# Layer 0's cross-attention: the reciprocals of the softmax sums moved behind the second pair's maxima

## The chip, the cores and the metric

The kernel runs on one core of a Trainium2 chip. The metric is device time in microseconds (us) of one execution; three executions of the kernel before were timed and their median is the number to compare with. A separate execution was profiled, and every duration below comes from that one. The engines are named as in the profile: PE (matrix multiplies), PEld (weight loads of the same engine), DVE (vector engine), ACT (scalar engine), POOL (GpSimd) and SP (issues DMAs).

## The reference, cut to what matters

The model is a two-layer decoder on `x` of shape (32, 100, 256) with a context `ctx_512` of shape (32, 361, 128). Each layer has a self-attention, a cross-attention and a feed-forward part. Only layer 0's cross-attention is touched:

```python
def _L0_xattn_ref(x, z, Wq, Wkv, Wo):          # 16 heads of 16 channels
    Q = (x @ Wq.T).reshape(B, xN, 16, 16)
    KV = (z @ Wkv.T).reshape(B, zN, 2, 16, 16)
    K, V = KV[:, :, 0], KV[:, :, 1]
    attn = jnp.einsum('bqhd,bkhd->bhqk', Q, K) * 16 ** -0.5
    attn = jax.nn.softmax(attn, axis=-1)
    O = jnp.einsum('bhqk,bkhd->bqhd', attn, V).reshape(B, xN, 256)
    return O @ Wo.T

x = x + _L0_xattn_ref(_layernorm(x), ctx_512, L0_xattn_Wq, L0_xattn_Wkv, L0_xattn_Wo)
```

For each of the 32 batches there are 16 heads, 100 queries and 361 context positions. The softmax needs the row maximum over the 361 positions, the exponentials, their sum, and a division of the weighted values by that sum.

## The kernel before, in words

`l0_xattn` treats a batch in two steps of eight heads each, so there are 64 steps, numbered `M` from 0; step `M` is batch `M // 2`, half `c = M % 2`. Eight heads are handled as two groups `j` of four heads. The loop is software-pipelined over three steps: in iteration `M` the scores of step `M` are computed and their maxima taken, the transposed scores and exponentials of step `M - 1` are made, and the values of step `M - 2` are summed and divided.

PE's order is the order written in the loop (a manual schedule). In one iteration PE does:

1. `maxima(M - 1)`: two transposes (L621), after which DVE adds the negated maxima to the queries (L623, tile `q`, here called the add of the maxima).
2. `scores(M, 0)`: four score matmuls into four PSUM banks; DVE takes the negated maximum of each bank with one reduction (L614). This is the first half.
3. `turned(M - 1, 0)`: twelve matmuls into four banks that give the shifted scores transposed; ACT takes four exponentials (L635), and POOL adds the three context chunks of the exponentials (L639, L640, tile `es`), for the sums.
4. `values(M - 2)`: 24 matmuls for the weighted values (L649) and 8 for the sums (L656), all into one bank. ACT copies the bank to SBUF (L661, tile `zs`), DVE takes the reciprocal of the sums (L662), POOL multiplies the values with it (L664, tile `zT`).
5. `scores(M, 1)` with four more reductions on DVE (L614): the second half.
6. `turned(M - 1, 1)` with four exponentials and POOL's two adds.
7. The extras, in the order 0, 2, 1 of a list of three: for `c = 0` the first keys of the next batch (`keys`, two ACT copies L586), the output projection of a finished tile of 128 rows, where there is one (`out`: DVE's add L241, then BN statistics L177 and L180), and two chunks of the next batch's values (`vals`, four ACT copies L599); for `c = 1` the other keys, the queries of the next four batches in every other pair of batches (`queries`, two ACT copies L579), and the last chunk of values. After them, in some steps, come the turn of a normalised tile (`norm_turn`, its copy L130 on ACT or L131 on DVE by turns) and the gate and routing work of the next feed-forward part, whose small operations run on DVE (L1401 to L1465).

All of this shares eight PSUM banks under one tag, handed out in turn. A matmul group gets the bank that was handed out eight banks earlier, and waits until that one has been read. Counted in that order, the keys take the bank of the first score matmul of the second half, so PE starts the keys only when DVE has done the first of the second half's four reductions; the second extra takes the bank of the second, and so on.

The engines other than PE run what was recorded for them in the order in which the program was built, each engine in order, waiting on the others by semaphores. On DVE the recorded order of one iteration before the change is: add of the maxima (L623), four reductions of the first half, the reciprocal (L662), four reductions of the second half, and then what the extras need (L241, L177, L180 or L131). On POOL it is: the two adds of `turned(M - 1, 0)`, the multiplication by the reciprocals (L664), the two adds of `turned(M - 1, 1)`. The helper `self.depend(instruction, [others], why)` adds a dependency that the data does not ask for.

Of the kernel before, what the change touches and what calls it, by code (L numbers as in the profile page):

```python
# [13 lines left out]
ALU = mybir.AluOpType  # L14
AX = mybir.AxisListType
# [64 lines left out]
class Kernel:  # L80
# [430 lines left out]
    def l0_xattn(self):  # L511
        nc, tc, a = self.nc, self.tc, self.a
        with ExitStack() as st:
# [54 lines left out]
            def load(b):  # L568
                ctx[b] = pool.tile([CD, LP], F32, tag="cT", name="cT", bufs=3)
                nc.sync.dma_start(ctx[b], a["ctxT"][:, b, :])  # L570

            def queries(b0, c):
                if c == 0:
                    q[b0 // 4] = pool.tile([P, 2, 2, 4 * T], F32, tag="qT", name="qT")
                pm = self.bank_t()[:, : 4 * T]
                self.mm(pm, [(wq[:, k, c * P : (c + 1) * P], self.xn_of(k, b0, 4)) for k in range(NK)])
                t = q[b0 // 4]
                for j in range(2):
                    nc.scalar.activation(t[:, c, j, :], pm, AF.Copy, scale=quarter[:, j : j + 1])  # L579

            def keys(b, c):
                pm = self.bank_t()[:, :L]
                self.mm(pm, [(wk[:, c * P : (c + 1) * P], ctx[b][:, :L])])
                t = ks[b % 3]
                for j in range(2):
                    nc.scalar.activation(  # L586
                        t[:, c, j, :L], pm, AF.Identity, bias=one[:, j : j + 1], scale=own[:, j : j + 1]
                    )

            def vals(b, c0, n):  # L590
                pm = self.bank_t()[:KC, : n * D].rearrange("p (c d) -> p c d", c=n)
                for i in range(n):
                    c = c0 + i
                    self.mm(pm[:, i, :], [(ctx[b][:, c * KC : (c + 1) * KC], wv)])
                pv = pm.rearrange("p c (h j d) -> p c h j d", j=2, d=16)
                v = vs[b % 3][:, c0 : c0 + n].rearrange("p c (h j) e -> p c h j e", j=2)
                for j in range(2):
                    for i in range(n):
                        nc.scalar.copy(v[:, i, :, j, 16 * j : 16 * j + 16], pv[:, i, :, j, :])  # L599

            def rows_of(r):
                return slice(32 * r, 32 * r + 32)


            def scores(M, j):
                b, c = divmod(M, 2)
                cols = slice((b % 4) * T, (b % 4 + 1) * T)
                ps = [self.bank("r")[:T, :L] for _ in range(4)]
                for r in range(4):
                    self.mm(ps[r], [(q[b // 4][rows_of(r), c, j, cols], ks[b % 3][rows_of(r), c, j, :L])])  # L610
                m = ms[M % 3]
                for r in range(4):
                    o = 32 * r + 16 * (1 - j)
                    nc.vector.tensor_reduce(m[:, j, o : o + 1], ps[r], AX.X, ALU.max, negate=True)  # L614

            def maxima(M):
                b, c = divmod(M, 2)
                cols = slice((b % 4) * T, (b % 4 + 1) * T)
                pt = self.bank_t()[:, : 2 * T].rearrange("p (j t) -> p j t", j=2)
                for j in range(2):  # L620
                    nc.tensor.transpose(pt[:, j, :], ms[M % 3][:, j, :], self.ident[:T, :T])  # L621
                q2[M] = pool.tile([P, 2, T], F32, tag="q2", name="q2")
                self.after = nc.vector.tensor_tensor(q2[M], pt, q[b // 4][:, c, :, cols], ALU.add)  # L623

            def turned(M, j):
                b, c = divmod(M, 2)
                ps = [self.bank("r")[:KC, : NKC * T] for _ in range(4)]
                for i in range(NKC):
                    for r in range(4):
                        self.mm(ps[r][:, i * T : (i + 1) * T], [(  # L630
                            ks[b % 3][rows_of(r), c, j, i * KC : (i + 1) * KC], q2[M][rows_of(r), j, :]
                        )])
                t = e[M, j] = pool.tile([KC, 4, NKC, T], F32, tag="e", name="e", bufs=5)
                for r in range(4):
                    nc.scalar.activation(t[:, r], ps[r].rearrange("p (c t) -> p c t", c=NKC), AF.Exp)  # L635

                n = L - 2 * KC
                s = es[M, j] = pool.tile([KC, 4, T], F32, tag="es", name="es", bufs=4)
                nc.gpsimd.tensor_tensor(s, t[:, :, 0, :], t[:, :, 1, :], ALU.add)  # L639
                nc.gpsimd.tensor_tensor(s[:n], s[:n], t[:n, :, 2, :], ALU.add)  # L640

            def values(M):
                b, c = divmod(M, 2)
                pz = self.bank_t()[:, : 2 * T].rearrange("p (s t) -> p s t", s=2)
                for j in range(2):
                    t = e.pop((M, j))
                    for i in range(NKC):
                        for r in range(4):
                            nc.tensor.matmul(  # L649
                                pz[rows_of(r), 0, :], lhsT=vs[b % 3][:, i, 8 * c + 2 * r + j, :],  # L650
                                rhs=t[:, r, i, :], start=(j == 0 and i == 0), stop=(j == 1 and i == NKC - 1),
                            )
                for j in range(2):
                    t = es.pop((M, j))
                    for r in range(4):
                        nc.tensor.matmul(  # L656
                            pz[rows_of(r), 1, :], lhsT=ones[:, j, :], rhs=t[:, r, :],
                            start=(j == 0), stop=(j == 1),
                        )
                zs = pool.tile([P, 2, T], F32, tag="zs", name="zs")  # L660
                nc.scalar.copy(zs, pz)  # L661
                nc.vector.reciprocal(zs[:, 1, :], zs[:, 1, :])  # L662
                for z, cols in self.z_parts(b):
                    nc.gpsimd.tensor_tensor(z[:, c, :], zs[:, 0, cols], zs[:, 1, cols], ALU.mult)  # L664

# [17 lines left out]
            def extras(b):  # L683

                k0, k1, v0, v1, o, x = [None] * 6
                if b + 1 < NB:
                    k0, k1 = (lambda: keys(b + 1, 0)), (lambda: keys(b + 1, 1))
                    v0, v1 = (lambda: vals(b + 1, 0, 2)), (lambda: vals(b + 1, 2, 1))
                if b > 1 and tile_of(b - 2) is not None:
                    o = lambda: out(tile_of(b - 2))  # L690
                b0, i = b // 4 * 4, b % 4
                if i < 2 and b0 + 4 < NB:
                    x = lambda: queries(b0 + 4, i)
                return k0, v0, o, k1, v1, x
# [11 lines left out]
            with tc.manual_schedule(engines={mybir.EngineType.PE}):  # L706
                load(0)
                load(1)
                for c in range(2):
                    queries(0, c)  # L710
                for c in range(2):
                    keys(0, c)
                vals(0, 0, 2)
                vals(0, 2, 1)
                last = 2 * NB
                for M in range(last + 2):
                    b, c = divmod(M, 2)
                    if c == 0:
                        if b + 2 < NB:
                            load(b + 2)  # L720
                        ex = extras(b)
                    if 0 < M <= last:
                        maxima(M - 1)
                    if M in norms:
                        f, *at = norms[M]
                        f(*at)
                    for j in range(2):

                        if M < last:
                            scores(M, j)  # L730
                        if 0 < M <= last:
                            turned(M - 1, j)
                        if j == 0 and M > 1:
                            values(M - 2)
                    for i in (0, 2, 1):
                        if ex[3 * c + i]:
                            ex[3 * c + i]()
                    if M not in norms or len(later) > 3:
                        for _ in range(1 + (len(later) > 3)):
                            if later:  # L740
                                later.popleft()()
                out(NF - 1)
                while later:
                    later.popleft()()
# [1260 lines left out]
```

## Time and profile before

| quantity | value |
|---|---|
| median of three runs | 3155.25 us (3146.28, 3155.25, 3155.63) |
| profiled execution: its own time | 3155.59 us |
| profiled execution: span of the instructions | 3153.6 us |
| granted PE clock over the span | 0.981 |
| busy over the span: PE / PEld / DVE / ACT / POOL | 96% / 72% / 57% / 45% / 29% |
| layer 0's cross-attention in the trace | about 587 to 1092 us, 505 us |
| in that stretch, busy PE / PEld / DVE / ACT / POOL | 474.8 / 367.3 / 362.1 / 330.9 / 294.2 us |
| reciprocals L662 | 64, median 778 ns, first at 602.5 us, last at 1089.5 us |
| reductions L614 | 512, median 523 ns |

The profiled execution's own time lies 2.0 us above its span; that is what stands around the first and last instruction. In the stretch of 505 us PE is idle for about 30 us, and every other engine for much more.

### The profile page before, as it was taken

The numbers are of one execution on the slowest core, as the hardware profiler recorded it, in microseconds if no ns is written. First come the engines' busy times: TensorE is split into PE (matmuls) and PEld (weight loads), VectorE is DVE, ScalarE is ACT, GpSimd is POOL, SyncE is SP. The second block draws the span as 40 slices with busy tenths as digits, with TensorE's granted clock in tenths as the row PEclk, the third lists the DMA queues.
The fourth block names the chain that finished last, engine by engine and source line by source line (L and its number), as shares of the span: only waits on it lengthen the run. The fifth ranks groups of instructions, "written<-read, shape, count | busy, mean of one in ns | idle before, by whom it ended". The sixth has DMA issues, their size and how long they took to land. (4 is left out here: it accounts for less than half of the span.)

```text
span 3153.6 us, 67966 instructions
## 1 busy us (share of the span) xinstructions
PE 3013.7 (96%) x26832; PEld 2261.1 (72%) x26832; DVE 1811.1 (57%) x4686; ACT 1406.8 (45%) x4361; POOL 926.3 (29%) x1048
## 2 busy tenths in 40 slices
PE   8999999999999899999998999999999999998983
PEld 7777777677777658888875677777777777776572
DVE  6666666577777622222227876656666666665443
ACT  5555554566666511222232234545545555454220
POOL 3222221465555451000016420021211212122474
PEclk9999999999999999999998999999999999999996
DMA  8850000000000033554541000010000000000387
GB/s 311 305 197 1 1 1 1 18 14 14 14 14 14 16 129 132 202 192 179 201 153 55 14 5 6 8 41 24 15 11 11 11 11 10 9 10 15 109 204 183
DMA packets 130105, 225.86 MB, mean 72 GB/s; under 512 B 40525, under 2 KB 108421, under 8 KB 122992
## 3 DMA queue, kind: packets, MB, share of 16 engines
q1 hardware_dynamic: 98704, 127.32, 12.6%
q0 software_dynamic: 27792, 90.81, 8.8%
q8 instruction: 215, 3.52, 0.5%
q10 hardware_dynamic: 3280, 3.28, 0.3%
q14 instruction: 114, 0.93, 0.1%
HBM read 153.77 MB, written 113.61 MB: 85 GB/s over the span
## 5 line engine op out<-in xcount | busy, mean ns | idle before, releaser
L1651 POOL DMA_INDIRECT x_d<-xr,slot x200 | 194.5, 972 | 775.3 <-DVE kT L131 243.7
L444 ACT ACTIVATE wBx<-ps_t,m 100x361 f32<-100x361 f32 x512 | 280.8, 560 | 259.7 <-DVE m L441 234.2
L136 PE MATMUL ps_t<-xnT,wA 128*128 128x200 f32 x1536 | 300.6, 340 | 1.9 <-DMA wA<-in_wq 1.3
L136 PEld LDWEIGHTS ps_t<-xnT,wA 128*128 128x128 f32 x1536 | 260.0, 192 | 37.4 <-issue 19.5
L441 DVE TENSOR_REDUCE m<-ps_t 100x1 f32<-100x361 f32 x512 | 241.2, 526 | 79.3 <-PE ps_t L136 77.2
L136 PE MATMUL ps_t<-xT,w 128*128 128x256 f32 x1276 | 283.2, 381 | 0.7 <-ACT xT L130 0.7
L136 PEld LDWEIGHTS ps_t<-xT,w 128*128 128x128 f32 x1276 | 240.0, 190 | 41.7 <-issue 9.3
L614 DVE TENSOR_REDUCE m<-ps_t 100x1 f32<-100x361 f32 x512 | 235.5, 517 | 18.1 <-PE ps_t L136 18.0
L338 POOL TENSOR_TENSOR e<-e,rz 100x400 f32<-100x400 f32 x128 | 109.5, 856 | 407.1 <-DVE rz L337 397.6
L635 ACT ACTIVATE e<-ps_t 121x300 f32<-121x300 f32 x512 | 173.9, 426 | 123.5 <-PE ps_t L136 123.4
L334 ACT ACTIVATE e<-s,m 100x100 f32<-100x100 f32 x512 | 186.1, 365 | 20.8 <-DVE m L328 20.1
L136 PE MATMUL ps_t<-wA,zT 128*128 128x256 f32 x800 | 188.0, 388 | 3.8 <-DVE zT L883 3.0
L136 PE MATMUL ps_t<-kT,qT 64*100 64x361 f32 x1024 | 190.1, 488 | 0.9 <-ACT wBx L444 0.9
L639 POOL TENSOR_TENSOR es<-e 121x400 f32<-121x400 f32 x128 | 132.4, 1034 | 197.0 <-ACT e L635 196.8
L136 PE MATMUL ps_t<-cT,wA 128*128 128x361 f32 x512 | 188.5, 492 | 1.5 <-SPq L1250 1.5
L453 PEld LDWEIGHTS ps_t<-ident,wBx 100*121 100x121 f32 x1536 | 178.1, 186 | 12.7 <-issue 5.7
L136 PE MATMUL ps_t<-wA,cT 128*121 128x512 f32 x384 | 184.9, 593 | 0.6 <-ACT wBx L444 0.6
L453 PE MATMUL ps_t<-ident,wBx 100*121 100x100 f32 x1536 | 185.3, 270 | 0.0
L136 PEld LDWEIGHTS ps_t<-wA,zT 128*128 128x128 f32 x800 | 152.1, 193 | 33.3 <-issue 4.7
L1332 DVE TENSOR_TENSOR h<-ps_t,g 128x256 f32<-128x256 f32 x145 | 61.2, 425 | 199.4 <-ACT g L1331 199.4
L131 DVE COPY eT<-ps_t 121x300 f32<-121x300 f32 x339 | 146.7, 461 | 30.6 <-PE ps_t L453 26.4
L471 PE MATMUL ps_z<-eT,v 121*64 121x100 f32 x3072 | 161.0, 254 | 0.3 <-issue 0.3
(301 smaller groups left out, 5810.6 us busy)
## 6 DMA issues: line engine op xcount, KB each, us to landing
x_d<-fill SPq DMA_DIRECT2D x16, 1284.0 KB
we<-in_wexp SPq DMA_DIRECT2D x32, 384.0 KB
cT<-in_ctxT SPq DMA_DIRECT2D x64, 181.5 KB
xe<-x_d SPq DMA_DIRECT2D x32, 321.0 KB
xe_d<-zero SPq DMA_DIRECT2D x8, 1024.0 KB
xe<-xe_d SPq DMA_DIRECT2D x29, 256.0 KB
y_d<-y SPq DMA_DIRECT2D x29, 256.0 KB
sum<-fill SPq DMA_DIRECT2D x10, 640.0 KB
```

The costliest lines, as they stand in the source:

```text
L131: return self.nc.vector.tensor_copy(out, in_)
L136: self.nc.tensor.matmul(out, lhsT=l, rhs=r, start=(i == 0), stop=(i == n - 1))
L334: nc.scalar.activation(t[:, i, :], s[:, i, :], AF.Exp, bias=m[:, i : i + 1], accum_out=rz[:, i : i + 1])
L338: nc.gpsimd.tensor_tensor(t[:, h, :], t[:, h, :], self.last(rz[:, h], T), ALU.mult)
L441: lay.after = nc.vector.tensor_reduce(m, ps[i], AX.X, ALU.max, negate=True)
L444: nc.scalar.activation(t[:, :L], ps[i], AF.Exp, bias=m, accum_out=sums[b][:, h : h + 1])
L453: nc.tensor.transpose(pt[:, c, :], e[n, i][:, c * KC : (c + 1) * KC], self.ident[:T, :T])
L471: nc.tensor.matmul(out, lhsT=v, rhs=eT[n, i][:, c, :], start=first, stop=last)
L614: nc.vector.tensor_reduce(m[:, j, o : o + 1], ps[r], AX.X, ALU.max, negate=True)
L635: nc.scalar.activation(t[:, r], ps[r].rearrange("p (c t) -> p c t", c=NKC), AF.Exp)
L639: nc.gpsimd.tensor_tensor(s, t[:, :, 0, :], t[:, :, 1, :], ALU.add)
L1651: got = nc.gpsimd.indirect_dma_start(out=self.x1_d[:, :], out_offset=bass.IndirectOffsetOnAxis(ap=slot[:, j, k : k + 1], axis=0), in_=xr[: ...
```

## The change

The reciprocal and the multiplication that follows it leave `values` and become a function of their own, `divided`, which is called once both halves of the scores have been recorded. The reciprocal gets a dependency on the last reduction of the second half. In the last two iterations there are no scores any more, and there the order stays as it was. Nothing is added or left out in the computation.

```diff
@@ scores(M, j)
                 for r in range(4):
                     o = 32 * r + 16 * (1 - j)
-                    nc.vector.tensor_reduce(m[:, j, o : o + 1], ps[r], AX.X, ALU.max, negate=True)
+                    got = nc.vector.tensor_reduce(m[:, j, o : o + 1], ps[r], AX.X, ALU.max, negate=True)
+                return got
@@ values(M)
                 zs = pool.tile([P, 2, T], F32, tag="zs", name="zs")
                 nc.scalar.copy(zs, pz)
-                nc.vector.reciprocal(zs[:, 1, :], zs[:, 1, :])
+                return zs
+
+            def divided(M, zs, after):
+                b, c = divmod(M, 2)
+                got = nc.vector.reciprocal(zs[:, 1, :], zs[:, 1, :])
+                if after is not None:
+                    self.depend(got, [after.ins], "behind the maxima, whose banks are waited for")
                 for z, cols in self.z_parts(b):
                     nc.gpsimd.tensor_tensor(z[:, c, :], zs[:, 0, cols], zs[:, 1, cols], ALU.mult)
@@ the loop over M
                     for j in range(2):
-                        if M < last:
-                            scores(M, j)
+                        got = scores(M, j) if M < last else None
                         if 0 < M <= last:
                             turned(M - 1, j)
                         if j == 0 and M > 1:
-                            values(M - 2)
+                            zs = values(M - 2)
+                    if M > 1:
+                        divided(M - 2, zs, got)
```

In the built program this moves 62 of the 64 reciprocals on DVE from in front of the second half's four reductions to behind them. The order on PE, ACT, POOL and SP is the same as before, instruction by instruction.

## The prediction

> **What bounds the kernel.** I read the page first, for the bound and the place of the touched lines.
>
> ```profile
> PE 3013.7 (96%) x26832; PEld 2261.1 (72%) x26832; DVE 1811.1 (57%) x4686; ACT 1406.8 (45%) x4361; POOL 926.3 (29%) x1048
> L614 DVE TENSOR_REDUCE m<-ps_t 100x1 f32<-100x361 f32 x512 | 235.5, 517 | 18.1 <-PE ps_t L136 18.0
> ```
>
> PE bounds; DVE, which the change touches, is 57% busy, so what counts is PE's idle time that DVE ends. Second, the waits of PE from 590 to 1080 us (total us, times, longest):
>
> ```profile
> PE ps_t L136 <- DVE m L614: 21.7, 63, 1.8
> PE ps_t L649 <- DVE m L614: 2.7, 4, 0.9
> ```
>
> The first line is most of PE's 30 us idle in this stage, and comes about once per step. Third, the timeline, for where it lies. Columns: start, duration, engine, line, operation, and in brackets the idle time before and its releaser.
>
> ```profile
> 704.50 0.87 PE L136 MATMUL ps_t<-k,qT 32*100 32x361 f32 x8
> ...
> 708.04 0.42 DVE L241 TENSOR_TENSOR x_sb<-ps_t,x_sb 128x256 f32<-128x256 f32 x1 [0.52 <-PE ps_t L136]
> ...
> 708.97 0.87 PE L136 MATMUL ps_t<-k,qT 32*100 32x361 f32 x8
> 709.08 0.37 DVE L623 TENSOR_TENSOR q<-ps_t,qT 128x200 f32<-128x200 f32 x1
> ...
> 709.66 0.94 PE L136 MATMUL ps_t<-q,k 32*121 32x100 f32 x24
> 709.85 1.85 DVE L614 TENSOR_REDUCE m<-ps_t 100x1 f32<-100x361 f32 x4 [0.41 <-PE ps_t L136]
> ...
> 712.04 0.87 PE L136 MATMUL ps_t<-k,qT 32*100 32x361 f32 x8
> ...
> 712.58 0.78 DVE L662 RECIPROCAL zs<-zs 128x100 f32<-128x100 f32 x1 [0.88 <-ACT zs L661]
> 712.73 0.79 PE L136 MATMUL ps_t<-q,k 32*121 32x100 f32 x24
> ...
> 713.27 1.78 DVE L614 TENSOR_REDUCE m<-ps_t 100x1 f32<-100x361 f32 x4
> 713.54 1.36 ACT L635 ACTIVATE e<-ps_t 121x300 f32<-121x300 f32 x4 [0.99 <-PE ps_t L136]
> 713.80 0.30 PEld L136 LDWEIGHTS ps_t<-cT,wB 128*128 128x128 f32 x2 [0.45 <-DVE m L614]
> 713.80 0.87 PE L136 MATMUL ps_t<-cT,wB 128*128 128x361 f32 x2 [0.28 <-DVE m L614]
> 714.09 0.54 POOL L664 TENSOR_TENSOR zT<-zs 128x68 f32<-128x68 f32 x2
> ...
> 714.98 1.03 POOL L639 TENSOR_TENSOR es<-e 121x400 f32<-121x400 f32 x1 [0.35 <-ACT e L635]
> ...
> 716.66 0.37 DVE L623 TENSOR_TENSOR q<-ps_t,qT 128x200 f32<-128x200 f32 x1 [1.60 <-PE ps_t L621]
> ```
>
> To be seen: DVE waits 0.88 us for the copied sums, divides, and only then reduces the second half; PE, done with the turned matmuls, stands 0.28 us until the first reduction frees the keys' bank.
>
> **What the move frees.** In the first half the reductions begin 0.88 us after the score matmuls (708.97 to 709.85); in the second, behind the reciprocal, 1.23 us after (712.04 to 713.27). Without it they begin 0.35 us earlier, at 712.92. The first one's end is what the keys wait for (713.27 + 0.53 = 713.80); it would be 713.45, and the turned matmuls end at 713.52 (712.73 + 0.79). So the 0.28 us goes. Over the stage that is the wait row: 21.7 us. The longest wait (1.78 us, at 886 us) is an exception: there DVE is full of routing work, the reciprocal takes 885.17 to 885.93 and the reductions start at 885.86, so only 0.69 us goes and 1.1 us stays.
>
> **What the moved step meets on DVE.** The 62 reciprocals keep their 0.78 us each. Each starts when the four reductions end: 0.88 + 1.85 = 2.73 us after the second half's scores; it also gains a wait on DVE's own last reduction, which no row shows. Nearest rows: a dependent pair on DVE (BN statistics end at 708.93, its aggregate starts at 708.96) gives 0.03, the longest hand-over that I found from DVE to PE (748.75 to 748.90) 0.15. A wait can't gain. I take 0.02 to 0.03, the pair on one engine, and keep 0.15 for the range. So: reciprocal from 2.76 to 3.54. Queued behind it are the adds and copies of the extras and the add of the maxima (L623), for which the next turned matmuls wait. By kind of step, counted from the rows of the stage as if no step had two extras that bind:
>
> - 23 steps with an output projection (L241). Now L241 starts 3.54 us after the scores (704.50 to 708.04) after 0.52 us idle; that idle is the cover. Behind the reciprocal it can start at about 3.46 (successive DVE operations overlap by 0.08, as 713.27 against 713.36 shows), and PE's result is there at 3.54 - 0.28 = 3.26. So DVE now sets it, 0.08 earlier than today. L177, L180 and L623 follow, L623 ending near 4.87; with 0.15 to PE the turned matmuls start at 5.02 instead of 5.16: 0.14 is gained, not 0.28. Given back: 23 x 0.14 = 3.2. Without the cover each reciprocal would cost its whole 0.78.
> - 7 steps with DVE's copy of a turned tile (L131), now after 0.52 us idle at 747.79 for scores at 744.25, the same 3.54: gained 0.08 or 0.09. Given back: 7 x 0.19 = 1.3.
> - 7 steps with that copy on ACT (L130): from 699.11 to 702.14 ACT runs exponentials, key copies, value copies and this copy without waiting for PE, and the next turned matmuls wait for ACT. Nothing gained: 7 x 0.28 = 2.0.
> - 13 steps with query copies (L579, 28 in all, two per step, one step ahead of the first reciprocal): they start at 716.06, ACT was ready near 715.84. Gained 0.22. Given back: 13 x 0.06 = 0.8.
> - The other 12, and those with queries, have over 1 us of DVE idle before L623 (1.60 at 716.66).
>
> **What it meets on POOL.** POOL's order stays, so its multiplication waits for the later reciprocal and the second pair of adds (L639, L640) queues behind it. Reciprocal's end 3.54, hand-over 0.08 (1090.29 to 1090.37 at the stage's end), multiplication 0.54, adds 1.11 + 1.03: done at 6.30 us. PE's sums matmuls (L656) need them for their second half; in a short step these come 6.44 us after the scores (697.61 to 704.05), 6.16 after the gain, their second half 0.27 later: 6.43. The slack is 0.13 us; I charge 0.05 in each of 26 short steps, 1.3. The product `zT` feeds no transfer; `out` reads it an iteration later, so its delay of about 1.5 us is hidden there. SP's queue is not passed.
>
> **Two rules weighed.** Four reductions of 523 ns take 1.85 us from a cold start here, so each begins before the last has ended. The Trainium skill, VectorE: DVE Perf Modes, section The DRAIN you can't avoid, says that the next operation does not start until the pipe is empty. By it the four would take 2.09, each of the 30 steps above would lose 0.24 more, and the gain would be 4.8; the row decides. The idle before the keys is 0.28 by matmuls and 0.45 by weight loads in the same two rows. The skill's Perfetto Trace Analysis, section Identifying the Most-Contended Engine, holds matmul busy time a bad measure and goes by weight loads. That would raise the gain by up to 0.17 x 62 = 10.5; I go by the release, which moves 0.35 at most.
>
> **The sum.** 21.7 - 1.1 - 3.2 - 1.3 - 2.0 - 0.8 - 1.3 = 12.0 us. After the stage PE is 95% busy again (633.5 of 650 us from 1250 on) and waits little for transfers, so the gain should reach the end. The profiled execution took 3155.59 us, 0.34 over the median of the runs; less 12.0 it is 3143.6, on the median's scale 3143.3. I say 3143.5. About 0.3%, 9.5 us, is what a measurement of this kernel can tell from no change.
>
> **Rivals.**
> - Full recovery: ACT and DVE keep up in every step, and the values' waits (L649, 2.7 us) go as well: 24.4 us, 3131. For: no engine but PE is over 72% busy in the stage. Against: L241 and L131, worked out above. Chance 0.15.
> - The gap reappears: in all 50 steps with an extra, ACT or DVE paces the next turned matmuls, and only the 12 plain ones gain: 12 x 0.28 = 3.4, 3152. For: weight loads of the turned matmuls already wait for ACT. Against: ACT and DVE idle in most of these steps. Chance 0.20.
> - POOL becomes the bound, slower than before: the later reciprocal holds POOL, the second adds come late, PE stands before L656. It begins to cost when the sums come after 6.43 us and decides against the change beyond today's 6.44 + 0.27 = 6.71, that is 0.41 later than worked out. At 1 us later the 26 short steps lose 0.59 each, 15 us: 3170. For: slack of only 0.13. Against: every link has a row. Chance 0.12.
> - That the change doesn't move anything is excluded: the built program has 62 reciprocals behind the reductions and no other difference in order.
>
> **How the numbers follow.** The forecast has 0.53: 0.15 us for the new wait takes 30 x 0.12 = 3.6 from it (8.4 gained), ACT and DVE keeping up in half of the give-backs adds 4, so its own range is 3139 to 3147, and 0.06 of its 0.53 lies within 0.3%. Faster: 0.47 + 0.15 = 0.62. Same: 0.06 + 0.20 = 0.26. Slower: 0.12. The range runs from the full recovery, 3131, over the reappearing gap to a little above no change, 3157; it leaves out the slower case and the far end of the full one.
>
> **What would show it.** Right: the wait of PE on L614 falls from 21.7 to a few us; the second half's reductions start 0.88 us after their scores; L662 waits for nothing on ACT; L241 and L131 start without idle; POOL's L664 idles about 1 us for L662. Wrong: L656 waits for L640 in many steps, L623 ends later after its scores than today, or the wait on L614 stays.

## The result and the profile after

| | before | changed |
|---|---|---|
| median of 12 runs each, same chip | 3150.99 us (3145.43 to 3160.5) | 3150.64 us (3145.53 to 3158.8) |
| profiled execution: its own time / span | 3155.59 / 3153.6 us | 3150.49 / 3148.7 us |
| granted PE clock over the span | 0.981 | 0.982 |

The ratio of the times is 0.9998, with an interval of 0.9986 to 1.001, that is 4.4 us less to 3.2 us more. No change can be measured. The gain of 12 us that the prediction held for likeliest is not there, although nearly every step of its working can be found in the trace.

To see the touched stage alone I measure the "63 steps", from the first reduction (L614) of step 0 to the first reduction of step 63. Before it is 485.1 us, changed 481.6. In some executions PE runs at half its clock for 3.4 us somewhere in the stage. In step 0, where all these kernels do the same, that costs 6.54 - 4.90 = 1.64 us, and such stretches are taken out at that price. Before has one (at 886 us), changed has none, so the comparison is 483.5 to 481.6: the change gained 1.9 us of the 12.

The first view is the page of the changed kernel:

```profile
PE 3012.6 (96%) x26832; PEld 2257.4 (72%) x26832; DVE 1825.7 (58%) x4686; ACT 1404.1 (45%) x4361; POOL 924.2 (29%) x1048
L614 DVE TENSOR_REDUCE m<-ps_t 100x1 f32<-100x361 f32 x512 | 239.6, 524 | 89.0 <-PE ps_t L136 88.7
```

DVE has the same 4686 instructions as before and is busy 14.6 us longer (1811.1 before). The kernel computes the same on the same shapes, so some instructions became slower; this is the trail that the experiments follow. The reductions changed from 517 to 524 ns, which is 4.1 us in all, and their idle time before them, 18.0 us, is now 88.7: DVE is free and waits for the scores, as was intended.

The waits of PE from 590 to 1080 us (total us, times, longest):

```profile
PE ps_t L650 <- DVE m L614: 8.8, 9, 1.9
PE ps_t L136 <- DVE q L624: 3.0, 8, 0.5
PE ps_t L136 <- DVE m L614: 2.4, 5, 1.2
```

The row of 21.7 us is down to 2.4. But the values' matmuls (L650, L649 before) now wait 8.8 us in nine places where they waited 2.7 in four, and the turned matmuls wait 3.0 for the add of the maxima where they waited 1.1: 8.0 us have come back elsewhere. Nor do wait rows add up to the time. Over the 63 steps PE idles 27.0 us before and 17.0 changed, but for the same work it is busy 458.2 and then 464.6 us: 6.4 of the 10.0 us are back as longer matmul rows.

The timeline of the same two steps that the prediction shows (start, duration, engine, line, operation; idle time before and its releaser in brackets):

```profile
704.36 0.87 PE L136 MATMUL ps_t<-k,qT 32*100 32x361 f32 x8
...
707.90 0.36 DVE L241 TENSOR_TENSOR x_sb<-ps_t,x_sb 128x256 f32<-128x256 f32 x1
...
708.47 0.77 ACT L599 COPY v<-ps_t 121x128 f32<-121x128 f32 x4 [0.17 <-PE ps_t L136]
...
709.33 0.89 PE L136 MATMUL ps_t<-q,k 32*121 32x100 f32 x24
...
711.67 0.87 PE L136 MATMUL ps_t<-k,qT 32*100 32x361 f32 x8
...
712.35 0.79 PE L136 MATMUL ps_t<-q,k 32*121 32x100 f32 x24
...
712.55 1.85 DVE L614 TENSOR_REDUCE m<-ps_t 100x1 f32<-100x361 f32 x4 [1.27 <-PE ps_t L136]
...
713.14 0.88 PE L136 MATMUL ps_t<-cT,wB 128*128 128x361 f32 x2
...
714.50 0.78 DVE L667 RECIPROCAL zs<-zs 128x100 f32<-128x100 f32 x1
...
715.36 0.54 POOL L671 TENSOR_TENSOR zT<-zs 128x68 f32<-128x68 f32 x2 [1.50 <-DVE zs L667]
...
715.86 1.03 POOL L640 TENSOR_TENSOR es<-e 121x400 f32<-121x400 f32 x1
...
716.97 1.04 POOL L641 TENSOR_TENSOR es<-es,e 119x400 f32<-119x400 f32 x1
```

The second half's reductions start 0.88 us after their scores (711.67 to 712.55), and the keys' matmuls follow the turned ones without a gap (712.35 + 0.79 = 713.14). That is the gain that was sought in this step, and it is made. The last rows are the price: POOL idles 1.50 us for the reciprocal, and its two adds end 6.34 us after the scores, where before they began at 714.98 and ended about 5.1 us after.

### The profile page after: what moved, and what is told of

The parts are those of the page before. It is cut to its first block, busy times and chain, and to the rows that moved or that the text cites. A ratio compares the mean times of both kernels' runs of the same rounds, so it can differ in the third digit from the quotient of the medians.

```text
span 3148.7 us, 68024 instructions
## 1 busy us (share of the span) xinstructions
PE 3012.6 (96%) x26832; PEld 2257.4 (72%) x26832; DVE 1825.7 (58%) x4686; ACT 1404.1 (45%) x4361; POOL 924.2 (29%) x1048
## 5 line engine op out<-in xcount | busy, mean ns | idle before, releaser
L614 DVE TENSOR_REDUCE m<-ps_t 100x1 f32<-100x361 f32 x512 | 239.6, 524 | 89.0 <-PE ps_t L136 88.7
L131 DVE COPY eT<-ps_t 121x300 f32<-121x300 f32 x339 | 146.6, 461 | 30.4 <-PE ps_t L453 26.4
L640 POOL TENSOR_TENSOR es<-e 121x400 f32<-121x400 f32 x128 | 132.3, 1034 | 92.1 <-ACT e L636 91.8
```

Of the source, the lines that this page charges most:

```text
L131: return self.nc.vector.tensor_copy(out, in_)
L614: got = nc.vector.tensor_reduce(m[:, j, o : o + 1], ps[r], AX.X, ALU.max, negate=True)
```

## The experiments

Theory A, formed from the page's DVE row and the two timelines: POOL's adds, pushed about one microsecond later by the multiplication that waits for the reciprocal, now run beside small DVE operations of the next step (rows of the norm, L189, and routing operations), slow these down, and so take back what the earlier reductions gave. Theory B, the rival: the slower DVE operations are a side effect, and the gain is lost to the reciprocal itself, which now stands in front of the add of the maxima, the out-projection and the routing work on DVE.

e1 to e4 share one chip, where before has a median of 3127.88 us (11 runs); e5 and e6 another (one run of before, 3149.19); e7 a third (3127.01, 11 runs). The profile of before is the one of the result above, from none of these runs. Ratios are against before on the same chip, and the 63 steps compare profiled executions. Where no edit acts, the traces of all the chips agree: step 1 takes 7.30 us in all nine. A single run has no interval, so of e3 to e6 only the stage is read.

| kernel | median us (runs) | ratio | 63 steps | less half-clock stretches | against 483.5 |
|---|---|---|---|---|---|
| changed | 3150.64 (12) | 0.9998 [0.9986, 1.001] | 481.6 | 481.6 | -1.9 |
| e1 | 3135.37 (6) | 1.0028 [1.0015, 1.004] | 491.7 | 490.1 | +6.6 |
| e2 | 3110.02 (5) | 0.9954 [0.994, 0.9968] | 471.7 | 471.7 | -11.8 |
| e3 | 3133.23 (1) | | 488.4 | 483.4 | -0.1 |
| e4 | 3105.73 (1) | | 470.2 | 468.5 | -15.0 |
| e5 | 3131.95 (1) | | 471.8 | 470.2 | -13.3 |
| e6 | 3133.47 (1) | | 468.1 | 466.5 | -17.0 |
| e7 | 3119.24 (7) | 0.997 [0.9959, 0.9981] | 481.3 | about 470 | about -14 |

### POOL late, and nothing else

e1 is the kernel before with every order as it was; the reciprocal stays in front of the second half's reductions. Only POOL's multiplication waits for the last of these.

```diff
...
                 nc.vector.reciprocal(zs[:, 1, :], zs[:, 1, :])
+                return zs
+
+            def divided(M, zs, after):
+                b, c = divmod(M, 2)
                 for z, cols in self.z_parts(b):
-                    nc.gpsimd.tensor_tensor(z[:, c, :], zs[:, 0, cols], zs[:, 1, cols], ALU.mult)
+                    got = nc.gpsimd.tensor_tensor(z[:, c, :], zs[:, 0, cols], zs[:, 1, cols], ALU.mult)
+                    if after is not None:
+                        self.depend(got, [after.ins], "behind the maxima")
...
```

> The order on every engine is that of the kernel before; only POOL's multiplication (zT) also waits for the last reduction of the second half, so that POOL is held about 1.0 us longer and its second adds end about 5.8 us after the second half's scores instead of 5.1 (6.3 in the changed kernel). Theory A (the late reciprocal holds POOL, whose second adds then run beside DVE's norm rows L189 and routing adds and make them up to three times as long): the 30 norm rows take about 18 us in all instead of 14.3 (23.1 in the changed kernel), and the stretch from the first L614 to the end of the last reciprocal is 503 to 507 us instead of 502.8. Theory B (the reciprocal delays DVE's queue by its own 0.78 us, POOL doesn't matter): 14.3 us and 502.8 within 0.5.

Measured: slower, 1.0028 with an interval of 1.0015 to 1.004; from the first reduction to the end of the last reciprocal 510.6 us, beyond the upper end of what A expected (502.8 before). The 30 norm rows take 22.0 us in all, 14.3 before. The waits of PE and of POOL in e1's stage:

```profile
PE ps_t L136 <- DVE m L614: 20.4, 59, 1.8
PE ps_t L650 <- DVE m L614: 8.9, 15, 1.3
```

```profile
POOL zT L669 <- DVE m L614: 74.5, 59, 2.6
```

The keys' wait of before is untouched (20.4 us), so nothing of the gain is here, and the values' wait has risen to 8.9 us, as in the changed kernel. POOL idles 74.5 us in front of the multiplication, which by itself costs nothing; what follows it does. The later POOL alone costs 6.6 us. Theory B has no place for that.

### The changed kernel with POOL's adds first

e2 is the changed kernel with one dependency more: the multiplication waits for the second pair of adds, so the adds no longer queue behind an instruction that waits for the reciprocal.

```diff
...
-                nc.gpsimd.tensor_tensor(s[:n], s[:n], t[:n, :, 2, :], ALU.add)
+                return nc.gpsimd.tensor_tensor(s[:n], s[:n], t[:n, :, 2, :], ALU.add)
...
-                    nc.gpsimd.tensor_tensor(z[:, c, :], zs[:, 0, cols], zs[:, 1, cols], ALU.mult)
+                    got = nc.gpsimd.tensor_tensor(z[:, c, :], zs[:, 0, cols], zs[:, 1, cols], ALU.mult)
+                    if after is not None:
+                        self.depend(got, [added.ins], "behind the second adds")
...
-                            turned(M - 1, j)
+                            added = turned(M - 1, j)
-                        divided(M - 2, zs, got)
+                        divided(M - 2, zs, got, added)
...
```

> The changed kernel with one thing more: on POOL the second adds come before the multiplication, so they don't wait for the late reciprocal. DVE's, PE's and ACT's orders are those of the changed kernel. Theory A: the norm rows fall from 23.1 to about 15 us, PE's waits of L650 on L614 from 8.8 to about 3 us, the stretch from 499.2 to 490 to 493 us, the time by about 10 us against the kernel before (ratio 0.996 to 0.998). Theory B: norm rows and the waits stay, 499 us, ratio 1.000.

Measured: 0.9954 with an interval of 0.994 to 0.9968, that is 10 to 19 us faster than before, and 9.9 us less than the changed kernel in the 63 steps. The ratio is below what A expected (0.996 to 0.998). It leaves nothing out of the computation and is faster than both kernels. The 30 norm rows take 16.7 us, PE's waits of L650 on L614 are 3.7. The rows of the norm tiles `wAn` from 590 to 1080 us tell the difference (minimum/median/maximum in ns), in the order before, changed, e1, e2:

```profile
L189 DVE TENSOR_SCALAR wAn<-x_sb,mv,rstd x21: 389/410/1140, 733.9 to 1065.5; 128x256 f32<-128x256 f32 x21
```

```profile
L189 DVE TENSOR_SCALAR wAn<-x_sb,mv,rstd x23: 389/646/1232, 732.7 to 1077.2; 128x256 f32<-128x256 f32 x23
```

```profile
L189 DVE TENSOR_SCALAR wAn<-x_sb,mv,rstd x21: 394/767/1185, 737.0 to 1072.2; 128x256 f32<-128x256 f32 x21
```

```profile
L189 DVE TENSOR_SCALAR wAn<-x_sb,mv,rstd x23: 390/414/1245, 731.3 to 1066.8; 128x256 f32<-128x256 f32 x23
```

The same instruction on the same shape: its median is 410 ns before, 646 and 767 where POOL is late, and 414 where the adds come early again. The minimum is the same everywhere, so it is not a slower engine but an encounter. One of them, in step 39, from the timeline of the changed kernel and then of e2 (whose steps lie 5.4 us earlier):

```profile
886.40 0.40 POOL L671 TENSOR_TENSOR zT<-zs 128x100 f32<-128x100 f32 x1 [2.75 <-DVE pos L1432]
...
886.71 2.34 DVE L189 TENSOR_SCALAR wAn<-x_sb,mv,rstd 128x256 f32<-128x256 f32 x2
...
886.76 1.03 POOL L640 TENSOR_TENSOR es<-e 121x400 f32<-121x400 f32 x1
...
887.87 1.03 POOL L641 TENSOR_TENSOR es<-es,e 119x400 f32<-119x400 f32 x1
```

```profile
881.13 0.40 POOL L671 TENSOR_TENSOR zT<-zs 128x100 f32<-128x100 f32 x1
...
881.30 0.74 DVE L189 TENSOR_SCALAR wAn<-x_sb,mv,rstd 128x256 f32<-128x256 f32 x2
...
883.72 1.03 POOL L640 TENSOR_TENSOR es<-e 121x400 f32<-121x400 f32 x1 [2.20 <-ACT e L636]
```

In the changed kernel two norm rows start while POOL multiplies and adds, and take 2.34 us; POOL's own operations keep their 1.03. In e2 the next adds come at 883.72, when the rows are long done, and the two take 0.74, though they start beside POOL's multiplication. The Trainium skill, SBUF — State Buffer, section Who interferes with whom, says that VectorE's copies, casts and tensor_scalar operations in their two-port modes, and its operations with two SBUF inputs, share a port pair with GpSimd, locked for a whole instruction, and that tensor_reduce on trn2 never takes part. The rows agree: L189 is a tensor_scalar and went from 0.40 to as much as 1.23 us, while the reductions' mean moved by 7 ns. That the port pair is the reason is the page's account; the experiments show only what the encounters cost.

### The adds first without the change

e3 is the kernel before with only POOL's adds put first; the reciprocal stays where it was.

```diff
...
+            def divided(M, zs, after, added):
...
+                    if after is not None:
+                        self.depend(got, [added.ins], "behind the second adds")
...
```

> The kernel before, with POOL's second adds before the multiplication and nothing else moved: the reciprocal stands where it stood. Both theories: the keys' wait of 21.7 us stays and the stretch is 502.8 within 1 us; if it falls by more, the order on POOL is worth something by itself and e2's gain is not the reciprocal's.

Measured: 63 steps of 488.4 us with three half-clock stretches, 483.4 without, against 483.5. The keys' wait stays at 21.3 us, and the norm rows take 14.0 us (14.3 before). The adds' place is worth nothing by itself, so e2's 11.8 us are the change's own gain, not one that the order on POOL brings: on one and the same chip e2 lies 11.7 us below e3. This run is also one that ties the chips together: with no effect to measure, it gives the same 63 steps on its chip as before on that of the result. Its whole time of 3133.23 us lies 5.4 above the median of before on its chip; the two half-clock stretches that it has more in the stage make 3.3 of that, the rest stays open.

### What the reciprocals themselves cost

e4 is the changed kernel without reciprocals; it leaves out the division, in all 64 steps.

```diff
-                got = nc.vector.reciprocal(zs[:, 1, :], zs[:, 1, :])
-                if after is not None:
-                    self.depend(got, [after.ins], "behind the maxima, whose banks are waited for")
```

> The changed kernel without the 62 reciprocals: the values are multiplied by the sums as they are, as soon as ACT has copied them. It leaves out the division. It prices what a reciprocal on DVE gives back in any place: by the forecast's terms for ACT (2.0 and 0.8 us) and for the routing step (1.1) the stretch is 485 us (502.8 less 21.7, plus 3.9). If DVE's place were free of cost, e2 would reach the same; by the forecast's terms e2 stays about 4.5 us above it (3.2 and 1.3 us).

Measured: 468.5 us, 15.0 less than before, and e2 lies only 3.2 us above it. So with POOL's adds out of the way the reciprocals, 64 x 0.78 = 50 us of DVE time, cost 3.2 us; DVE's idle time covers the rest. The prediction gave back 3.2 + 1.3 = 4.5 us for their new place in front of L241 and L131. That closes theory B: the reciprocal's place on DVE costs no more than was charged for it.

### The norm rows on another engine

e5 and e6 move the norm rows from DVE to ScalarE and leave out the subtraction of the mean in them; e5 does so in the changed kernel, e6 in e2. What is routed later differs by that, so their whole times say nothing, only the stage is read.

```diff
...
+    def norm_row_act(self, f, out):
+        return self.nc.scalar.activation(out, self.x[:, f, :], AF.Identity, scale=self.norms[f][1])
...
-                xn = self.norm_rows(f, n, after=self.after)
+                xn = self.norm_rows(f, n, after=self.after, eng="act")
...
```

> The changed kernel (POOL's order as in it, so POOL is held by the late reciprocal), with the stage's norm rows (30 of L189) on ScalarE instead of DVE. It leaves out the subtraction of the mean in these rows, so later routing differs and only the stage is read. Measure: from the first L614 of step 0 to the first of step 63, 481.6 us in the changed kernel and 471.7 with POOL's adds first (e2). If POOL's hold costs because the norm rows on DVE collide with the adds, 472 to 475 us, and PE's waits of L650 on L614 fall from 8.8 to under 5 us. If the hold costs by another way (PE waiting for the sums, the reciprocal ahead of the reductions), 479 to 483.

> The same edit on top of POOL's adds first (e2); it leaves out the same subtraction. If the collision with the norm rows is the whole cost of the hold, this and e5 agree within 2 us, near 470 to 473; otherwise e5 stays 6 us or more above this one.

Measured: 470.2 us for e5 and 466.5 for e6, both below what was expected. PE's waits of the values' matmuls on the reductions, 8.8 us in the changed kernel, are gone from e5's list. Without norm rows on DVE the changed kernel loses 11.4 us of its 481.6, e2 only 5.2 of its 471.7; the difference, 6.2 us, is what POOL's delay costs through the norm rows. But e5 and e6 were expected to lie within 2 us, and they lie 3.7 apart. The rest is in steps 23 and 31 (1.1 us each) and some others, the steps with routing work. The operation `sel` of step 23 in the changed kernel and in e2:

```profile
757.29 0.90 DVE L1420 TENSOR_TENSOR sel<-hot,hot 128x16 f32<-128x16 f32 x1
```

```profile
755.22 0.16 DVE L1422 TENSOR_TENSOR sel<-hot,hot 128x16 f32<-128x16 f32 x1
```

An operation on 16 elements with two SBUF inputs takes 0.90 us instead of 0.16; POOL's add L640 runs from 757.13 to 758.16 beside it. The cast of four elements shortly before takes 0.88 instead of 0.24. So the 9.9 us between the changed kernel and e2 are about 6.2 for norm rows and 3.7 for the rest, of which the routing operations are the part that I found in the rows; I did not remove them by themselves.

### The norm rows on ScalarE, whole

e7 is e2 with the whole norm row on ScalarE: two one-column operations make the bias, minus the mean times the reciprocal deviation, and a third makes the row.

```diff
...
+        nc.scalar.mul(t[:, 0:1], rstd, -1.0)
+        nc.scalar.activation(t[:, 1:2], mean, AF.Identity, scale=t[:, 0:1])
+        return nc.scalar.activation(out, self.x[:, f, :], AF.Identity, bias=t[:, 1:2], scale=rstd)
...
```

> POOL's adds first (e2), and the stage's norm rows on ScalarE with the mean subtracted by a bias of -mean x rstd, for which ScalarE does two operations of one column per tile (about 0.2 us each, 60 of them, 12 us in 505 us of a ScalarE that is 65% busy). By the collision: from the first L614 of step 0 to the first of step 63 it takes 467 to 471 us (466.5 without the bias and without a half-clock stretch, 471.7 with the rows on DVE), and against the kernel before 13 to 18 us are gained, ratio 0.994 to 0.996. If ScalarE, which now holds the exponentials back behind the rows, paces PE instead, it is no better than e2: 471 us or more.

Measured: 0.997 with an interval of 0.9959 to 0.9981. It is faster than before, but not by what was expected, and not better than e2. In steps 19, 35 and 51 it loses 4.14, 4.32 and 2.99 us against e2. The timeline and then the clock (window, us, busy time and instructions of PE, PEld, DVE, ACT and POOL, granted PE clock, DMA share, GB/s):

```profile
729.28 0.61 PE L136 MATMUL ps_t<-k,qT 32*100 32x361 f32 x1 [1.65 <-ACT e L647]
...
729.90 2.08 PE L136 MATMUL ps_t<-q,k 32*121 32x100 f32 x23
```

```profile
730.00:736.00 6.00, 6.00 (x32) 3.96 (x31) 1.31 (x2) 2.94 (x8) 4.65 (x6) 0.50 0.01 4
```

ACT's eight one-column operations take 1.36 us (726.13 to 727.49) between two loads of its tables of 1.28 us each, the exponentials stand behind them, PE waits 1.65 us for these, and behind that pause PE works at half its clock for 6 us: 23 of the turned matmuls take 2.08 us where 24 took 0.79 in the changed kernel. In its 63 steps e7 had 24 us at half clock; without them it would lie near 470, 2 us better than e2. That is worked out from the price of a stretch, not shown.

## Why the prediction was right and wrong

Right, in the order of its steps:

- **What the move frees.** The wait of PE on the reductions went from 21.7 to 2.4 us; 19.3 of the 20.6 forecast are gone (21.7 less the 1.1 of the routing step). The reductions start 0.88 us after the scores.
- **What the moved step meets on DVE.** The reciprocal starts 2.83 us after the scores instead of 2.76: it begins 0.10 after the last reduction's end at 714.40. That is between the 0.02 to 0.03 taken and the 0.15 kept for the range. The add L241 starts without idle time, but at 3.54, no earlier than before (3.46 forecast), and the turned matmuls of that step 4.97 us after the scores (5.02 forecast, 5.16 before). There it is ACT's value copies that pace them, not the add of the maxima, but the gain of 0.19 is near the 0.14.
- **POOL's own times.** The multiplication starts at 3.69 and the adds end at 6.34, for a forecast of 3.54 + 0.08 = 3.62 and of 6.30. PE waits for the sums of POOL (L657 on L641) once, 1.0 us, at the end of the stage, as before the change (1.1). So neither the 1.3 charged for it nor the rival "POOL becomes the bound" came about.
- **The sum.** 12.0 forecast, 11.8 measured in e2, where the one thing is mended that the sum left out. That the two are so near is partly luck. The 23 steps with an output projection gain 4.2 us in e2 (3.2 forecast), the seven with ACT's copy of a turned tile 1.3 (nothing forecast), the seven with DVE's copy 0.25 (0.6 forecast; one step counts as both the first and the last kind), and the 1.3 for POOL is not lost.
- **The two rules.** The one that would have cut the gain to 4.8 (no operation before the pipe is empty) does not hold for these rows: four reductions still take 1.85 us. The section that the prediction cites for it goes on that an operation that is not held starts earlier, so it does not stand against the rows. The one that counts idle time by weight loads would have put the gain up to 10.5 higher, near 22; e2 gives 11.8, so the matmuls' row was the one to go by here. Its section speaks of how near PE is to its limit, not of the price of a single wait.

Wrong is the step "What it meets on POOL". It followed the delay of about 1 us along the data only: who waits for `es`, who waits for `zT`. It found 0.13 us of slack at the sums, and that was right. It did not ask which DVE operations stand at the place that the adds move to. The adds of 1.03 us then meet norm rows and routing operations of the next step and stretch them by up to 0.8 us each; the rest of the routing work and the next reductions queue behind these on DVE, and PE waits for them (the row of 8.8 us). The term that is missing from the sum is 481.6 - 471.7 = 9.9 us. The profile of before could have told. In the stretch around 886 us, of which the prediction says that DVE is full of routing work, the same addition on 128x8 takes 0.16 us when it starts ahead of POOL's add and 0.96 when it starts behind it:

```profile
882.99 0.16 DVE L1414 TENSOR_TENSOR acc<-acc,sel 128x8 f32<-128x8 f32 x1
883.06 1.07 POOL L639 TENSOR_TENSOR es<-e 121x400 f32<-121x400 f32 x1 [3.36 <-ACT e L635]
...
883.18 0.96 DVE L1414 TENSOR_TENSOR acc<-acc,sel 128x8 f32<-128x8 f32 x1
```

The losses lie mostly in steps with norm rows or routing work: step 23 lost 1.31 us against before, step 3 lost 0.87, step 31 lost 0.70, step 11 lost 0.64, while most steps with neither gained 0.09 to 0.34. Over the 63 steps, as measured, the gains sum to 10.0 and the losses to 6.5.

The likeliest case, with its own range of 3139 to 3147 us, is therefore the one that failed. That 3150.64 us lies within the stated range of 3131 to 3157 is luck: the range reached that far for the sake of a rival, and what happened is none of the cases that the prediction weighed. The measured time, 0.4 us below before, has the size of the rival "the gap reappears", but by another mechanism: the gap before the keys did not reappear, and ACT did not pace the plain steps. What was forecast as its "wrong if" signs (L656 waiting for L640, L623 ending later in many steps, the wait on L614 staying) shows only in part: the wait on the add of the maxima rose from 1.1 to 3.0 us, and as it is 3.0 in e2 as well, it is not what cost the 9.9. The sign that told the story was one that the prediction did not list, the busy time of DVE at an unchanged count of instructions. It points to a place and gives no price: in e2 DVE is still busy 7.4 us longer than before (1818.5).

## What to carry to other kernels

When a change makes one engine's work later, ask not only who waits for its result but what runs beside it in its new place; here a DVE operation of 0.16 us that met one of POOL's adds took 0.90. A step in an in-order queue that is made to wait should stand behind the work that is ready: one dependency that put the adds first turned a change of no effect into one of 10 to 19 us. After a run, compare each engine's busy time at equal instruction counts first, since a rise there is work that got slower, not work that was added, and then look for what runs beside it.

## What the runs showed of the hardware

- Beside POOL's adds, DVE operations can stretch, by kind: a norm row (tensor_scalar, 128x256) from 0.40 to as much as 1.23 us, a product of two SBUF inputs (128x16) from 0.16 to 0.90, a cast (128x4) from 0.16 to 0.88. The reciprocal (0.78 us), the reductions (0.52) and the BN statistics (0.43) keep their times, and POOL's adds keep their 1.03.
- The reciprocal starts 0.10 us after the end of the reduction that it is made to wait for (714.40 to 714.50, and the same wherever it follows one in the changed kernel's 63 steps), the BN statistics 0.03 after the add that they read (708.26 to 708.29), while independent DVE operations overlap by 0.08.
- Pauses of PE of 1.65 us (e7) and 1.78 us (before, at 886 us) were followed by half clock for 3.4 to 6.8 us. The Trainium skill, TensorE: Matmul & The Clock Gate, section HAM oscillation — how this bites in real kernels, puts the limit at pauses over about 3.4 us. These rows differ from it, and the measurement decides. But the same pause of 1.78 us in e1 (at 892 us) and pauses of 1.15 and 1.93 us in step 39 of the changed kernel were followed by none, and e3 has half clock from 856.5 us with no pause over 0.33 us in the 3.5 us before it. So the length of the pause is not what decides alone, and what else does stays open.
